# Conv of every second band's fourth channel block: diagonal half-channel weights in four array tiles instead of composite weights

## The chip, the cores and the metric

The kernel runs on one core of a Trainium2 chip. The time is device microseconds from launch to end; before the change the median of three runs is 3966.65 us (3966.45 to 3969.41). Engines: PE (matrix products, with PEld its weight loads), DVE (vector), ACT (activations and copies), POOL (GpSimd) and SP (DMA queue).

## The reference

One transformer-like layer on 16 images of 128 channels and 96 x 96 pixels, fp32: channel attention with a residual, then this feed-forward part with a residual.

```
xn2 = layernorm over channels of x
h1  = w_in (512 x 128) applied to each pixel of xn2
h2  = 3 x 3 depthwise conv of h1, 512 channels, zero padding
h3  = gelu(h2)
out = x + w_out (128 x 512) applied to each pixel of h3
```

## The kernel before

An image is cut into 8 bands of 12 rows (BR = 12), so there are 128 bands, numbered g. The 512 hidden channels are four blocks of 128 (n = 0 to 3). Channels lie on the 128 partitions, pixels along the free dimension. A normalised image lies in the ring `xn`, rows padded by one column.

A pair (g, n) is a job of `conv_job`, in the usual way: PE projects the rows into PSUM (`hidden`, L1162, mostly 4 rows or 384 columns at a time), ACT copies them into the padded buffer `h1s[n]` (`kept`, L1167), and the two rows that the next band needs are copied at the end (`halo`, L1158), so that they aren't projected twice. The nine taps are then shared out. ACT makes two to four products (L1178, tile `pr`); POOL adds one of them to the unscaled middle tap (`merge`, L1181) and issues DMAs that add another product to a product (L1203) and the rest to the result (L1206). DVE does the other taps as multiply-adds over 1152 pixels in the PSUM tile `acc` (L1194; L1190 the first and the last). ACT applies GELU (L1211) into `h3`.

For 45 of the 128 bands (`PE_BANDS`, `PE_LAST`) the fourth block (n = 3, `PE_CHUNK`) goes another way, `by_matmuls`: PE computes projection and conv at once from `xn`, with nine composite matrices `comp[:, t, :]` (w_in times the tap's weight, 128 x 128), for units of 4 rows: nine matmuls into one PSUM bank (L1274) and a small one of six rows that corrects the columns at the image's edge (L1280). ACT applies GELU from PSUM (L1292). These bands need no projection, copy or halo for n = 3.

`ffn_out` multiplies by w_out, four matmuls for 4 rows (L1315), and DVE adds them to x (L1322). Beside this run the norms and the attention of the next image: transposes (L868, L964), mixing (L818), Gram sums (L916), statistics on DVE (L876), scales on POOL (L881, L885, L909). All PE results but Gram and `acc` pass through four PSUM banks, `h_0` to `h_3`.

The order on each engine is fixed when the program is built. `Plan` gives each operation a place on a common axis of jobs (`at(kind, place)`, with offsets `AT`, and `SHIFTS` by stretch of 15 jobs) and costs in ns, and plays the work through; of the operations that are ready, each engine takes the one with the lowest place.

Of the kernel before, what the change touches and what calls it, by code (L numbers as in the profile page):

```python
# [21 lines left out]
PE_OF = 30
PE_LAST = (0, 1, 3, 4, 6)
# [28 lines left out]
    load_w=-385.3, weights=-616.15, zeros=-141.7, load_a=-42.4, forth_a=-588.2, stats_a=1671.35, variance_a=269.75,  # L52
    power_a=-755.3, pool_product=152.05, merge=-380.8, scaled_a=-1419.9, gram=1191.75, back_a=416.05,
    place_a=228.35, attention=-37, mix=1454.35, residual=-779.15, mixed=-33.8, add_x=-342.3, forth_b=1585.15,
    stats_b=614.45, variance_b=-1160.25, power_b=-1398.6, shift_b=20.9, scaled_b=-3615.05, back_b=417.3,
    place_b=-902.15, halo=4531.85, hidden=416.95, kept=-903.15, products=3487.6, add_last=-380.1, tap=10.85,
    add_first=-1420.85, gelu=4569.5, conv=1192.9, conv_gelu=10.15, out=421.1, add=612.75, store=75.2,
    mix_0=-440.15, residual_0=-785.8, mixed_0=-1036.75, add_x_0=-1518.55, gram_0=475.45, forth_a_0=-103.4,
    forth_b_0=-946.85, stats_a_0=-789.15, stats_b_0=-710.05, scaled_a_0=-915.5, copied_a=35.4, copied_b=-38.35,
    copied_a_0=-43.45, copied_b_0=1111, scaled_b_0=-128.2, back_a_0=485, back_b_0=-1340.55, place_a_0=-547.95,  # L60
    place_b_0=-708.95, shift_b_0=22.8, late=-293.55, load_a_0=-390.35, load_dw=-378, units=-654.05,
# [5 lines left out]
    0: dict(load_w=1.9, zeros=-8.4, load_a=-22.8, forth_a=-1.1, stats_a=-0.3, variance_a=-0.3, power_a=-8.1,
        merge=-300.7, gram=0.2, back_a=-0.2, place_a=-1660.1, attention=-276.4, mix=-21.7, residual=-23.2,
        mixed=530.5, forth_b=40.5, stats_b=-118.7, variance_b=14.1, power_b=605.1, back_b=0.1, place_b=1.6,
        halo=4.3, kept=986.6, products=-7.1, add_last=329.8, tap=-1.6, add_first=1.7, gelu=7.1, conv=-6,  # L70
        conv_gelu=0.4, out=0.2, add=-660.9, store=1.7, mix_0=-899, residual_0=-622, gram_0=0.9, forth_a_0=18.5,
        stats_a_0=-2.4, stats_b_0=19.6, scaled_a_0=-65.5, copied_a=-60.9, back_a_0=-6.5, back_b_0=0.2,
        place_a_0=399.7, place_b_0=1296.2, late=10.6, load_a_0=4.4, load_dw=229.6, units=8.6, variance_a_0=619.5,
        power_a_0=-469.8, variance_b_0=-341, power_b_0=-17.1),
    1: dict(load_a=-14.5, forth_a=0.1, stats_a=14.8, variance_a=1354, power_a=1176.9, merge=637, scaled_a=46.3,
        gram=-0.1, back_a=0.1, place_a=1.6, attention=-12.1, mix=-4.5, mixed=403.6, add_x=1946.3, forth_b=-6.6,
        stats_b=-1.9, variance_b=-52.3, power_b=5.8, back_b=170.3, place_b=-0.2, halo=-1066.6, hidden=-3.3,
        kept=923, products=1, add_last=-6.7, tap=0.7, add_first=1488, gelu=1.5, conv=0.7, conv_gelu=0.9, out=-0.4,
        add=2.8, copied_a=379.4),
    2: dict(forth_a=0.2, stats_a=-3.5, variance_a=-8.2, merge=0.8, scaled_a=-9.6, gram=3281.1, place_a=1229.9,  # L80
        mixed=38.9, forth_b=-125.8, stats_b=576.6, variance_b=-252.3, power_b=-0.5, back_b=-1367.9, place_b=-21.3,
        halo=-1033.7, kept=0.2, add_last=1838.5, add_first=19.2, gelu=-95.7, conv=-0.2, conv_gelu=0.1, add=-688.1,
        store=-2.9, copied_b=-10.5),
    3: dict(load_a=0.3, stats_a=-421.1, variance_a=1.7, power_a=1940.7, merge=360.1, scaled_a=19.9, gram=-3.7,
        back_a=-1.6, place_a=-1386.7, mix=-3.2, mixed=-1368.8, add_x=331.4, forth_b=9.5, stats_b=-631.1,
        power_b=84.1, place_b=-406.8, halo=-5.4, kept=976.7, products=0.3, add_last=0.8, tap=0.1, add_first=1358.3,
        gelu=2.1, conv=-2.9, conv_gelu=-0.3, add=-1929.6, store=-1489.9, copied_a=4.3),
    4: dict(load_a=-0.5, forth_a=0.4, stats_a=-0.7, power_a=24.6, merge=-2.2, scaled_a=1377.6, back_a=-152.2,
        place_a=-15.7, mixed=-9.8, add_x=2.6, forth_b=73.3, stats_b=12.2, variance_b=-15.1, power_b=-8.5,
        back_b=0.1, place_b=2076.2, halo=5, kept=185.5, products=-0.1, add_last=6.5, tap=0.5, add_first=-10.8,  # L90
        gelu=-13.4, conv=-3.1, conv_gelu=0.7, out=0.1, add=-664.4, store=1113.3, copied_a=-1138.6),
    5: dict(load_a=0.1, stats_a=-1.1, variance_a=-313.3, power_a=1.2, merge=-12.5, scaled_a=1035.8, gram=-3.2,
        back_a=-3.1, place_a=-265.5, attention=-0.6, mix=2.8, mixed=137.1, add_x=-6.9, forth_b=-29.6,
        stats_b=-638.6, variance_b=771.6, power_b=45, back_b=-404.6, place_b=146, halo=-0.5, kept=200.1,
        add_last=2.7, add_first=-1.7, gelu=-2, conv=0.4, conv_gelu=0.3, add=2.9, store=1134, copied_a=1.4,
        copied_b=18.3),
    6: dict(forth_a=-0.2, stats_a=15.7, variance_a=-46.9, power_a=976.2, scaled_a=-8.2, gram=2277.6, back_a=-2,
        place_a=-7.5, mix=0.1, mixed=-346.5, add_x=-1.2, forth_b=3.4, stats_b=0.2, variance_b=0.1, power_b=37.6,
        back_b=-0.5, place_b=1358.9, halo=49.9, kept=-465.7, products=-0.1, gelu=21, conv=-22.3, conv_gelu=0.1,
        add=-599.3, store=3342.4, copied_a=-381.6),  # L100
    7: dict(forth_a=0.2, stats_a=-1.6, variance_a=1309.9, power_a=2424.9, merge=0.2, scaled_a=4976.2, gram=-27.8,
        back_a=11.1, place_a=176.5, attention=-0.4, mix=0.7, mixed=-5.3, add_x=358.3, forth_b=7.9, stats_b=1.4,
        variance_b=-1.7, power_b=8.5, back_b=0.6, place_b=19.7, halo=1.9, kept=864.1, products=-1, add_last=342.7,
        tap=-0.6, add_first=15.3, gelu=5, conv=3346, conv_gelu=-0.5, store=1090.3, copied_a=-967.2,
        copied_b=1704.6),
    8: dict(load_a=-2.4, forth_a=1.3, stats_a=0.3, variance_a=-4.2, power_a=-4.3, merge=7.7, scaled_a=670.4,
        gram=2291.6, place_a=24.6, mix=-0.3, mixed=1600.2, add_x=-36.8, forth_b=57.3, stats_b=1042.9,
        variance_b=-17, power_b=-0.3, back_b=-0.2, place_b=2469.7, halo=-2888.4, kept=1099.2, add_last=-33.7,
        tap=0.8, gelu=-6.8, conv=-6.2, conv_gelu=0.9, out=0.1, add=-406.4, copied_a=2.7),
    9: dict(load_a=-1.9, stats_a=-0.2, variance_a=-0.1, power_a=23.8, merge=-25, scaled_a=11.3, gram=-7.9,  # L110
        back_a=-0.3, place_a=-511.8, attention=-1.8, mix=-2.4, mixed=-1119.9, add_x=320.8, forth_b=-16.7,
        stats_b=-566.6, variance_b=8.9, power_b=10.1, back_b=-0.2, place_b=-0.8, kept=-0.8, products=-0.3,
        add_last=-16.7, tap=0.3, add_first=6.8, gelu=19.2, conv=-5.3, conv_gelu=0.1, add=0.7, store=-980.3,
        copied_a=25.1),
    10: dict(forth_a=-0.1, stats_a=-18.6, variance_a=213.9, power_a=-1.6, merge=-0.3, scaled_a=1679, gram=3360.3,
        back_a=-0.8, place_a=-13.6, mix=-3.6, mixed=503.8, add_x=829.5, forth_b=1.4, stats_b=16.4,
        variance_b=1422.9, power_b=15, back_b=0.5, place_b=1532, halo=9, hidden=1.3, kept=1393.5, products=0.1,
        add_last=-363.1, add_first=-14.8, gelu=10.8, conv=0.2, out=67.7, store=-4.8, copied_a=-32.2,
        copied_b=-331.3),
    11: dict(forth_a=-0.7, stats_a=13.2, variance_a=367, power_a=5322.9, merge=-21.3, scaled_a=1837.4, gram=3416.9,  # L120
        back_a=-339.2, attention=-1, mix=-1.1, mixed=640.8, add_x=2.6, forth_b=4.6, stats_b=10.1, variance_b=-16.9,
        power_b=4.6, back_b=-0.2, place_b=565.6, halo=13.3, hidden=-0.7, kept=859.2, add_last=23.5, tap=0.7,
        add_first=-6.9, conv=1.5, conv_gelu=-0.2, add=1024.5, store=4493.9),
# [1276 lines left out]
```

## Time and profile before

| | us |
|---|---|
| median of three runs | 3966.65 |
| span of the profiled execution | 3974.3 |
| PE busy | 3892.4 |
| DVE busy | 3834.8 |
| ACT busy | 3558.1 |
| POOL busy | 3379.4 |

The profiled execution's own time is its span. PE's busy time counts matmuls whose ends are modelled and overlap, so that the pace of matmuls is read from their starts. Groups of the profile give an operation's line, output and inputs, shape, count, then busy time and mean ns of one, then the idle time before it and what ended it.

### The profile page before, as it was taken

The numbers are of one execution on the slowest core, as the hardware profiler recorded it, in microseconds if no ns is written. First come the engines' busy times: TensorE is split into PE (matmuls) and PEld (weight loads), VectorE is DVE, ScalarE is ACT, GpSimd is POOL, SyncE is SP. The second block draws the span as 40 slices with busy tenths as digits, with TensorE's granted clock in tenths as the row PEclk, the third lists the DMA queues.
The fourth block names the chain that finished last, engine by engine and source line by source line (L and its number), as shares of the span: only waits on it lengthen the run. The fifth ranks groups of instructions, "written<-read, shape, count | busy, mean of one in ns | idle before, by whom it ended". The sixth has DMA issues, their size and how long they took to land.

```text
span 3974.3 us, 50973 instructions
## 1 busy us (share of the span) xinstructions
PE 3892.4 (98%) x16760; PEld 2521.7 (63%) x16760; DVE 3834.8 (96%) x4390; ACT 3558.1 (90%) x5186; POOL 3379.4 (85%) x3107
## 2 busy tenths in 40 slices
PE   8999999999999999999999999999999999999999
PEld 7566666666666666666666666666666666665555
DVE  7999999999999999999999999999999999999998
ACT  3989989989999999999989989999899999998886
POOL 5998988898898988988888888888888888888674
PEclk9999999999999999999999999999999999999999
DMA  3999999999999999999999999999999999999996
GB/s 100 187 191 204 200 200 198 199 202 198 210 201 209 203 198 203 200 210 201 194 202 197 207 201 194 205 197 206 189 192 206 203 207 201 203 197 183 191 189 146
DMA packets 191691, 777.42 MB, mean 196 GB/s; under 512 B 22208, under 2 KB 23616, under 8 KB 191424
## 3 DMA queue, kind: packets, MB, share of 16 engines
q0 software_dynamic: 151920, 622.33, 82.6%
q1 hardware_dynamic: 38784, 151.75, 10.2%
q8 instruction: 132, 2.16, 0.2%
q14 instruction: 135, 1.11, 0.1%
q10 hardware_dynamic: 720, 0.07, 0.0%
HBM read 148.85 MB, written 75.50 MB: 56 GB/s over the span
## 4 chain that ended last, share of the span: by engine, by line
PE 58%; DVE 14%; ACT 10%; DMA 7%; POOL 6%; issue 5%; POOLq 0%; DVEq 0%; ACTq 0%
PE h L1315 15%; PE h L1162 14%; PE h L1274 13%; DVE acc L1194 6%; DMA h<-pr 5%; ACT pr L1178 5%; PE h L818 4%; PE h L964 4%; PE g L916 3%; PE h L868 3%; DVE acc L1190 3%; DVE h L1190 2%; ACT h L1167 2%; POOL merged L1181 2%; DMA pr<-pr 2%
## 5 line engine op out<-in xcount | busy, mean ns | idle before, releaser
L1178 ACT ACTIVATE pr<-h,ratio 128x1152 f32<-128x1152 f32 x1494 | 1837.2, 1271 | 37.6 <-DMA h<-pr 12.6
L1194 DVE SCALAR_TENSOR_TENSOR acc<-h,ratio,acc 128x1152 f32<-128x1152 f32 (+1 forms) x1308 | 1810.3, 1384 | 7.7
L1181 POOL TENSOR_TENSOR merged<-pr,h 128x1152 f32<-128x1152 f32 x466 | 1238.1, 2657 | 100.5 <-DVE acc L1190 54.7
L1162 PE MATMUL h<-xn,winT 128*128 128x384 f32 (+2 forms) x2802 | 1088.0, 496 | 16.0 <-ACT h L1167 9.2
L1315 PE MATMUL h<-h,woutT 128*128 128x384 f32 x3072 | 1086.2, 488 | 1.7 <-ACT h L1167 1.1
L1274 PE MATMUL h<-xn,comp 128*128 128x380 f32 (+2 forms) x2430 | 895.0, 482 | 2.2 <-ACT h L1167 1.5
L1167 ACT COPY h<-h 128x384 f32<-128x384 f32 (+2 forms) x1401 | 652.9, 493 | 192.4 <-PE h L1162 187.5
L1315 PEld LDWEIGHTS h<-h,woutT 128*128 128x128 f32 x3072 | 565.2, 190 | 359.3 <-ACT h L1167 7.8
L1162 PEld LDWEIGHTS h<-xn,winT 128*128 128x128 f32 x2802 | 500.0, 190 | 326.6 <-issue 34.2
L1190 DVE SCALAR_TENSOR_TENSOR acc<-h,ratio,merged 128x1152 f32<-128x1152 f32 x466 | 686.6, 1473 | 20.9 <-POOL merged L1184 10.1
L1206 POOL DMA_DIRECT2D h<-pr x466 | 463.3, 994 | 241.9 <-DVE h L1190 57.5
L1190 DVE SCALAR_TENSOR_TENSOR h<-h,ratio,acc 128x1152 f32<-128x1152 f32 x467 | 655.2, 1403 | 3.4
L1211 ACT ACTIVATE h<-h,ksum 128x1152 f32<-128x1152 f32 (+2 forms) x586 | 616.0, 1081 | 46.4 <-DMA h<-pr 45.6
L1274 PEld LDWEIGHTS h<-xn,comp 128*128 128x128 f32 x2430 | 430.6, 189 | 235.2 <-issue 17.1
L1203 POOL DMA_DIRECT2D pr<-pr x466 | 478.7, 1040 | 103.1 <-ACT pr L1178 73.4
L885 POOL TENSOR_TENSOR ve_b<-ve_b,mhalf 128x4 f32<-128x4 f32 x288 | 366.0, 1277 | 7.9
L909 POOL TENSOR_TENSOR zT<-zT,ve_a 128x512 f32<-128x512 f32 x270 | 331.3, 1232 | 8.6
L885 POOL TENSOR_TENSOR ve_a<-ve_a,mhalf 128x4 f32<-128x4 f32 x288 | 318.6, 1109 | 15.3
L868 PE MATMUL h<-ident,x 128*128 128x128 f32 x2244 | 317.0, 275 | 13.7 <-ACT xn L970 4.9
L868 PEld LDWEIGHTS h<-ident,x 128*128 128x128 f32 x2244 | 263.6, 142 | 96.4 <-issue 38.6
L818 PE MATMUL h<-xn,mwT 128*128 128x384 f32 x768 | 289.1, 490 | 7.7 <-ACT h L1167 3.2
L916 PEld LDWEIGHTS g<-zT 128*128 128x128 f32 x2160 | 269.9, 191 | 40.2 <-POOL zT L909 11.0
(190 smaller groups left out, 3967.0 us busy)
## 6 DMA issues: line engine op xcount, KB each, us to landing
pr<-pr POOLq DMA_DIRECT2D x466, 576.0 KB, 7.8
h<-pr POOLq DMA_DIRECT2D x466, 576.0 KB, 7.7
x<-in_x_dram SPq DMA_DIRECT2D x128, 576.0 KB, 7.5
out_dram<-x SPq DMA_DIRECT2D x127, 576.0 KB, 4.6
x<-in_x_dram POOLq DMA_DIRECT2D x123, 576.0 KB, 9.1
out_dram<-x SPq DMA_DIRECT2D x3, 192.0 KB, 1.9
h<-in_L_conv_w_in_dram SPq DMA_DIRECT2D x1, 256.0 KB, 3.4
h<-in_L_conv_w_out_dram SPq DMA_DIRECT2D x1, 256.0 KB, 3.6
```

Source lines behind the costliest of these rows:

```text
L868: nc.tensor.transpose(d["pT", q][:, k, :], xt[:, j * P : (j + 1) * P], ident)
L885: nc.gpsimd.tensor_tensor(rstd, rstd, mhalf, ALU.pow)
L1162: nc.tensor.matmul(rows(ph), lhsT=winT[:, n, :], rhs=window(xn, r0 + r, e - r, 1), start=True, stop=True)
L1167: nc.scalar.copy(window(h1_, r, e - r, 1), rows(d.pop(("ph", r))))
L1178: nc.scalar.activation(to, shifted(t), AF.Copy, scale=ratio[:, n, t : t + 1])
L1181: nc.gpsimd.tensor_tensor(merged, d["pr", dma_taps[0]], shifted(UNIT), ALU.add)
L1190: nc.vector.scalar_tensor_tensor(to, shifted(t), ratio[:, n, t : t + 1], also, ALU.mult, ALU.add)
L1194: nc.vector.scalar_tensor_tensor(to, shifted(t)[:, lo:hi, cut], ratio[:, n, t : t + 1], to, ALU.mult, ALU.add)
L1203: nc.gpsimd.dma_start(out=d["pr", dma_taps[1]], in_=d["pr", t], accum_op=ALU.add)
L1211: nc.scalar.activation(h3, h3, AF.Gelu, bias=ksum[:, z, n : n + 1])
L1274: nc.tensor.matmul(d["pc"][:, lo:hi, cut], lhsT=comp[:, t, :], rhs=window(xn, r0 + dy, UR, dx)[:, lo:hi, cut], start=(t == order[0]), stop ...
L1315: nc.tensor.matmul(rows(d["po"]), lhsT=woutT[:, n, :], rhs=h3s[g, n][:, s * UR : (s + 1) * UR, :], start=(k == 0), stop=(k == NCH - 1),)
```

## The change

`by_pe` now takes every second band (64 of 128: `PE_OF = 2`, the odd g). In those bands the fourth block is projected, copied and passed on by the halo copy like the others (kinds `hidden_p`, `kept_p`, `halo_p`); only the conv itself goes over PE. Its weights `diag` are diagonal, nine taps of 64 x 64 for each half of the channels. The array is used as four tiles of 64 rows and 64 columns: row half m is the half of the channels, column half q the half of the band's rows (q = 0 rows 0 to 5, q = 1 rows 6 to 11). In two steps (k) of 3 rows (288 columns) each tap takes four matmuls, (q, m) = (0, 0), (1, 1), (1, 0), (0, 1), into two PSUM banks, one for each m, so that a bank holds 64 channels of two row groups. GELU reads a bank (`ksum_pe` holds the bias in that layout), and `h3` of this block keeps the layout.

`ffn_out_pe` therefore starts a unit of 3 rows with matmuls on half the partitions (`wout_pe`, tiles of 64 x 128, one row half for each of two output banks) and then adds the other three blocks with full matmuls. The edge correction (L1280) and the composite matrices are gone. All offsets are new: `AT`, `TURN`, and `PHASES` by the band's place in the image, while `SHIFTS` is empty.

```diff
-PE_BANDS = (0, 3, 6, 9, 12, 15, 18, 21, 24, 27)
-PE_OF = 30
-PE_LAST = (0, 1, 3, 4, 6)
+PE_BANDS = (0,)
+PE_OF = 2
+HALF = 64
+PR = 3
...
-    comp = const.tile([P, 9, P], F32, name="comp")
+    diag = const.tile([P, 9, HALF], F32, name="diag")
...
+            pe(t_mm((e - r) * W), at("hidden" + pe_, jk), lambda r=r, e=e: hidden(r, e), [*zs, ("w", "in")], [ph, *to])
+            act(t_copy((e - r) * W), at("kept" + pe_, jk), lambda r=r, e=e: kept(r, e), [ph], to)
+        if pe_:
+            by_matmuls(j, g, h1)
+            if to_halo:
+                act(t_copy(2 * W), at("halo_p", j), halo, h1[3:], h1[:1])
+            return
...
+    def by_matmuls(p, g, h1):
+        order = (1, 0, 2)
+
+        def product(k, dy):
+            if dy == order[0]:
+                d["pc", k] = [rows(bank((g, "conv", k, m), PR * W)) for m in range(2)]
+            for dx in (1, 0, 2):
+                t = 3 * dy + dx
+                for q, m in ((0, 0), (1, 1), (1, 0), (0, 1)):
+                    r0 = 2 * PR * q + PR * k
+                    lo, hi, _ = inside(t, b * BR + r0, PR, True)
+                    of, to = slice(m * HALF, (m + 1) * HALF), slice(q * HALF, (q + 1) * HALF)
+                    nc.tensor.matmul(
+                        d["pc", k][m][to, lo:hi, :], lhsT=diag[of, t, :],
+                        rhs=window(h1s[PE_CHUNK], r0 + dy, PR, dx)[of, lo:hi, :],
+                        start=(t == UNIT), stop=(dy == order[-1] and dx == 2),
+                    )
...
+        def gelu(k, m):
+            for a, e, z in step_parts(k):
+                to = h3_of(g, PE_CHUNK)[:, 2 * PR * m + PR * k + a : 2 * PR * m + PR * k + e, :]
+                nc.scalar.activation(to, d["pc", k][m][:, a:e, :], AF.Gelu, bias=ksum_pe[:, z, m : m + 1])
...
+    def ffn_out_pe(p, g, k):
+        pos = [("h", ("out", g, q, k)) for q in range(2)]
+        r0s = [2 * PR * q + PR * k for q in range(2)]
...
+        def halves():
+            for m in range(2):
+                for q in range(2):
+                    of = slice(q * HALF, (q + 1) * HALF)
+                    r = 2 * PR * m + PR * k
+                    nc.tensor.matmul(
+                        rows(bank(pos[q][1], PR * W)), lhsT=wout_pe[of, m, :], rhs=h3s[g, PE_CHUNK][of, r : r + PR, :],
+                        start=(m == 0), stop=False,
+                    )
```

PE's order in the middle of the run, before: a unit of a band whose fourth block goes over PE. A row is line, operation, output and inputs (`x_...` and `ve_b...` belong to the norms, `mwT` to the mixing), shape and how many in a row.

```order
L1274 MATMUL h_3_76<-xn_128,comp_124 128x384
L1274 MATMUL h_3_76<-xn_128,comp_124 128x4x95
L818 MATMUL h_0_73<-xn_128,mwT_8_12948 128x384
L1274 MATMUL h_3_76<-xn_128,comp_124 128x4x95 x3
L818 MATMUL h_0_73<-xn_128,mwT_8_12948 128x384
L818 MATMUL h_2_75<-xn_128,mwT_8_12948 128x384
L1274 MATMUL h_3_76<-xn_128,comp_124 128x384
L1274 MATMUL h_3_76<-xn_128,comp_124 128x4x95
L1280 MATMUL h_3_76<-ident_78,edgeT_112 128x4x2
```

The composite matmuls of a unit, in one bank, are mixed with other work and close with the edge matmul. On PE after the change, at the second step of such a band's conv (L1094 is the projection, L1259 the full output products, L798 and L894 transposes, L846 the Gram sums):

```order
L1094 MATMUL h_0_73<-xn_127,winT_121 128x384
L1259 MATMUL h_2_75<-h3_6_159,woutT_122 128x384
L894 MATMUL h_3_76<-ident_78,ve_b7_8_14071 128x128 x3
L846 MATMUL g_8_13220<-zT_2_163 128x129 x4
L1094 MATMUL h_0_73<-xn_127,winT_121 128x384
L1094 MATMUL h_3_76<-xn_127,winT_121 128x384
L798 MATMUL h_1_74<-ident_78,x2_7_4_13962 128x128 x4
L1211 MATMUL h_2_75<-h1_3_143,diag_123 64x288
L1211 MATMUL h_0_73<-h1_3_143,diag_123 64x288
```

The two banks `h_2` and `h_0` then take 24 such matmuls without a break, one other operation, and the last 12; over the whole run there are 217 unbroken runs of 12, 24 or 36. On PE, at the output of that band (L1283 works on half the partitions):

```order
L748 MATMUL h_0_73<-xn_127,mwT_7_13212 128x384
L1283 MATMUL h_2_75<-h3_2_155,wout_pe_83 128x288
L1283 MATMUL h_1_74<-h3_2_155,wout_pe_83 128x288
L1283 MATMUL h_2_75<-h3_2_155,wout_pe_83 128x288
L1283 MATMUL h_1_74<-h3_2_155,wout_pe_83 128x288
L1259 MATMUL h_2_75<-h3_0_153,woutT_122 128x288
L1259 MATMUL h_2_75<-h3_7_160,woutT_122 128x288
L1259 MATMUL h_2_75<-h3_3_156,woutT_122 128x288
L1259 MATMUL h_1_74<-h3_0_153,woutT_122 128x288
```

Two output banks are now filled together, where `ffn_out` before filled one with four full matmuls. On ACT, after the change, around a band of the next image (L1110 products, L1227 the GELU of PE's blocks, L1143 that of the others, L1090 the halo copy; `h1_3` is the fourth block's buffer):

```order
L1110 ACTIVATE pr_1_146<-h1_1_141,ratio_106 128x1152
L1143 ACTIVATE h3_2_155<-h3_2_155,ksum_110 128x1152
L1090 COPY h1_2_142<-h1_2_142 128x2x96
L1227 ACTIVATE h3_0_153<-h_3_76,ksum_pe_111 128x288
L1055 COPY mwT_8_15033<-g_8_13220 128x128
L1056 COPY d_8_15035<-g_8_13220 128x1
L1227 ACTIVATE h3_0_153<-h_1_74,ksum_pe_111 128x288
L1090 COPY h1_3_143<-h1_3_143 128x2x96
L1110 ACTIVATE pr_4_149<-h1_1_141,ratio_106 128x1152
```

Each step's two banks are emptied by two GELUs, and the fourth block's halo copy, which before was left out beside a band that went over PE, now follows the first step. Over the run ACT's copies of projected rows go from 1401 to 1536, halo copies from 371 to 448, products from 1494 to 1437.

More of the change, by code (lines that the diff above doesn't have):

```diff
@@ L51 @@
 AT = dict(
[L52 to L61, printed above, removed]
@@ new lines @@
+    variance_b=2.39, power_b=2.49, shift_b=22.37, scaled_b=-3613.23, back_b=3.21, place_b=3.36, halo=6.59,
+    halo_p=8.94, hidden=3.5, hidden_p=5.31, kept_p=3.82, kept=1.97, products=10.49, add_last=6.26, tap=5.39,
+    add_first=6.31, gelu=7.45, conv=8.06, conv_gelu=8.64, out=6.8, add=7.23, store=5.08, mix_0=7.87,
+    residual_0=13.83, mixed_0=-1036.57, add_x_0=-1522.05, gram_0=11.4, forth_a_0=13.33, forth_b_0=4.32,
+    stats_a_0=15.56, stats_b_0=8, scaled_a_0=16.57, copied_a=-4.84, copied_b=3.43, copied_a_0=-42.25,
@@ new lines @@
+    copied_b_0=1111.46, scaled_b_0=-128.12, back_a_0=18.85, back_b_0=13.55, place_a_0=17.71, place_b_0=11.05,
+    shift_b_0=31.15, late=10.9, load_a_0=12.46, load_dw=15.58, units=9.96, variance_a_0=13.17, power_a_0=21.5,
+    variance_b_0=8.5, power_b_0=11.24,
+)
+TURN = dict(
+    load_w=-386.6, weights=-616.15, zeros=-121.87, load_a=-42.46, forth_a=-595.61, pool_product=152.05,
+    attention=-36.46, mix=1452.66, products=3498.48, tap=10.94, conv=13.45, conv_gelu=10.15, mix_0=-440.15,
+    forth_a_0=-103.4, load_a_0=-400.68,
+)
@@ L65 @@
 STRETCH = 15
 SHIFTS = {
[L67 to L123, printed above, removed]
-    12: dict(load_a=10.3, forth_a=5.5, stats_a=9.9, variance_a=-0.8, merge=-188.3, gram=0.1, place_a=-1371.9,
-        mix=-1.2, mixed=-1155.8, add_x=-847.4, forth_b=-21.3, stats_b=581.5, variance_b=21.3, power_b=-52.5,
-        place_b=1.1, halo=-3.3, kept=17.6, products=0.4, tap=1, add_first=9.7, gelu=14.3, conv=-0.1, out=-0.4,
-        add=959.9, store=-103.4, copied_a=-1417.6),
@@ L194 @@
-    29: dict(merge=964.3, mix=2.3, mixed=29.9, add_x=-554.8, forth_b=-404.1, stats_b=2866.7, variance_b=1165.5,
-        power_b=2005.5, back_b=-405.9, place_b=13.1, hidden=-0.1, kept=-2.5, products=-0.2, add_last=968.5,
-        gelu=-4545.7, conv=-5.1, conv_gelu=-1.8, out=170.1, add=-604.8, store=0.5, copied_b=3518.7),
-    30: dict(merge=0.3, mix=32.8, mixed=-2.3, add_x=956.2, forth_b=9.3, stats_b=-10.1, variance_b=787.8,
-        power_b=0.4, back_b=-0.3, place_b=-44.2, halo=-4106.2, kept=-4.5, products=-1.5, add_last=7.5,
-        add_first=-1.5, gelu=-14.8, conv=0.1, conv_gelu=-0.1, add=-2030, store=-448.6),
@@ L200 @@
-    31: dict(merge=4987, hidden=741.3, kept=1.8, products=1119.8, tap=1184.1, add_first=2628.9, gelu=-4553.7,
-        conv=9, conv_gelu=-2.6, out=4185.8, add=-1517.3, store=4532.1),
 }
-STEP = dict(scaled=0.3, hidden=0.1, products=0.5, tap=0.166, conv=1.6, conv_tap=0.03, out=0.8, out_part=0.05)
+STEP = dict(scaled=0.3, hidden=0.1, products=0.5, tap=0.166, conv=1.6, conv_tap=0.03, out=0.8, out_pe=1.2, out_part=0.05)
 SLACK = 150
@@ L477, in tile_restormer_block @@
     ksum = const.tile([P, 3, NCH], F32, name="ksum")
[L478 to L479 removed]
+    ksum_pe = const.tile([P, 3, 2], F32, name="ksum_pe")
     none = const.tile([P, 1], F32, name="none")
@@ L706, in keep_centred_in @@
                 nc.vector.tensor_mul(ksum[:, z, :], ksum[:, z, :], kn)
-                for side in range(2):
-                    to = edge[:, 2 * z + side : 2 * z + side + 1]
-                    nc.vector.tensor_reduce(to, ratio[:, PE_CHUNK, lo + 2 * side : hi : 3], AX.X, ALU.add)
-            nc.vector.tensor_scalar(edge, edge, kn[:, PE_CHUNK : PE_CHUNK + 1], -1.0, ALU.mult, ALU.mult)
-        def edges():
-            v["pe"] = bank(("weights", "edge"))[:6, :P]
-            nc.tensor.transpose(v["pe"], edge, ident)
-        def centred_conv(ts):
-            pc = v["pc4"] = bank(("weights", "centred conv", ts[0]))[:, : len(ts) * P]
-            nc.tensor.matmul(
-                pc, lhsT=centre, rhs=comp[:, ts[0] : ts[-1] + 1, :].rearrange("p t c -> p (t c)"), start=True, stop=True
-            )
+            for q in range(2):
+                for m in range(2):
+                    of, to = ksum[m * HALF : (m + 1) * HALF, :, PE_CHUNK], ksum_pe[q * HALF : (q + 1) * HALF, :, m]
+                    nc.vector.tensor_copy(to[:, :1], of[:, :1])
+                    nc.vector.tensor_copy(to[:, 1:2], of[:, 1:2] if not q else of[:, :1])
+                    nc.vector.tensor_copy(to[:, 2:], of[:, 2:] if q else of[:, :1])
         def unit_parts():
@@ L753, in weights @@
         dve(3300, at("late", p), keep_centred_in, pc + pk, [("w", "in")])
-        pk = [("h", ("weights", "edge"))]
-        pe(230, at("late", p), edges, [("w", "in")], pk)
-        dve(200, at("late", p), lambda: nc.vector.tensor_copy(edgeT, v["pe"]), pk, [("w", "conv")])
         transposed(
@@ L1148, in conv_job @@
         jn = (g, n)
-        from_halo = b > 0 and (n != PE_CHUNK or not by_pe(g - 1))
-        to_halo = b < NB - 1 and (n != PE_CHUNK or not by_pe(g + 1))
+        from_halo = b > 0
+        to_halo = b < NB - 1
+        pe_ = "_p" if j is None else ""
+        j = first[g] if pe_ else j
         h1_ = h1s[n]
@@ L1306, in ffn_out, with step_parts @@
-    def ffn_out(p, g, s):
+    def by_matmuls(p, g, h1):
         i, b = divmod(g, NB)
         d = {}
-        po = ("h", ("out", g, s))
-        order = sorted(range(NCH), key=lambda n: (n != PE_CHUNK, n))
-        def product(k, n):
-            if k == 0:
-                d["po"] = bank(("out", g, s), UT)
-            nc.tensor.matmul(
-                rows(d["po"]), lhsT=woutT[:, n, :], rhs=h3s[g, n][:, s * UR : (s + 1) * UR, :],
-                start=(k == 0), stop=(k == NCH - 1),
-            )
-        def add_here():
-            xt = x_unit(xbs, i, s + b * UPB)
-            nc.vector.tensor_add(xt, d["po"], xt)
-        def store(k, n):
-            at_ = slice(b * BR * W + k * UT, b * BR * W + (k + n) * UT)
-            nc.sync.dma_start(out=ov[i, :, at_], in_=xbs[i, b][:, k * UT : (k + n) * UT])
+        order = (1, 0, 2)
[12 more added lines that the diff above has]
+                        start=(t == UNIT), stop=(dy == order[-1] and dx == 2),
+                    )
+        def step_parts(k):
+            if b == 0 and k == 0:
+                return [(0, 1, 1), (1, PR, 0)]
+            if b == NB - 1 and k == 1:
+                return [(PR - 1, PR, 2), (0, PR - 1, 0)]
+            return [(0, PR, 0)]
+        def gelu(k, m):
+            for a, e, z in step_parts(k):
+                to = h3_of(g, PE_CHUNK)[:, 2 * PR * m + PR * k + a : 2 * PR * m + PR * k + e, :]
+                nc.scalar.activation(to, d["pc", k][m][:, a:e, :], AF.Gelu, bias=ksum_pe[:, z, m : m + 1])
+        for k in range(2):
+            pcs = [("h", (g, "conv", k, m)) for m in range(2)]
+            h3 = [("h3", (g, PE_CHUNK), k)]
+            for c, dy in enumerate(order):
+                pk = p + STEP["conv"] * k + STEP["conv_tap"] * c
+                pe(T_CONV, at("conv", pk), lambda k=k, dy=dy: product(k, dy), [*h1[k:], ("w", "conv")], [*pcs, *(h3 if not c else ())])
+            ns = sum(t_act((e - a) * W, 1) for a, e, _ in step_parts(k))
+            for m in range(2):
+                act(ns, at("conv_gelu", p + STEP["conv"] * k), lambda k=k, m=m: gelu(k, m), [pcs[m]], h3)
@@ new lines, in out_add, with add_here, store @@
+    def out_add(p, g, key, r0, n):
+        i, b = divmod(g, NB)
+        units = range(r0 // UR, (r0 + n - 1) // UR + 1)
+        xt = lambda: xbs[i, b][:, r0 * W : (r0 + n) * W]
+        def add_here():
+            nc.vector.tensor_add(xt(), banks[plan.slot[key]][:, : n * W], xt())
+        def store(r0, n):
+            at_ = slice((b * BR + r0) * W, (b * BR + r0 + n) * W)
+            nc.sync.dma_start(out=ov[i, :, at_], in_=xbs[i, b][:, r0 * W : (r0 + n) * W])
+        dve(t_dve(n * W), at("add", p), add_here, [key], [("xb", (i, b), s) for s in units])
+        if g == NG - 1:
+            move(at("store", p), lambda: store(r0, n), [("xb", (i, b), s) for s in units], [], T_MOVE * n / BR)
+        elif r0 + n == BR:
+            move(at("store", p), lambda: store(0, BR), [("xb", (i, b), k) for k in range(UPB)], [], T_MOVE)
@@ L1328, in ffn_out, with product_of, product @@
+    def product_of(po, g, n, r0, e0, start, stop):
+        nc.tensor.matmul(rows(po), lhsT=woutT[:, n, :], rhs=h3s[g, n][:, r0:e0, :], start=start, stop=stop)
+    def ffn_out(p, g, s):
+        po = ("h", ("out", g, s))
+        order = range(NCH)
+        def product(n):
+            product_of(bank(po[1], UT), g, n, s * UR, (s + 1) * UR, n == 0, n == NCH - 1)
         for k, n in enumerate(order):
             pk = p + STEP["out_part"] * k
-            pe(t_mm(UT), at("out", pk), lambda k=k, n=n: product(k, n), [*(("h3", (g, m), s) for m in (order if k == 0 else [n])), ("w", "out")], [po])
@@ L1331, in ffn_out @@
-        band_ = [("xb", (i, b), k) for k in range(UPB)]
-        dve(t_dve(UT), at("add", p), add_here, [po], [("xb", (i, b), s)])
-        if g == NG - 1:
-            move(at("store", p), lambda: store(s, 1), [("xb", (i, b), s)], [], T_MOVE / UPB)
-        elif s == UPB - 1:
-            move(at("store", p), lambda: store(0, UPB), band_, [], T_MOVE)
+            pe(t_mm(UT), at("out", pk), lambda n=n: product(n), [*(("h3", (g, m), s) for m in (order if k == 0 else [n])), ("w", "out")], [po])
@@ L1348, in tile_restormer_block @@
     band = len(jobs) / NG
+    own = {gn: j for j, gn in enumerate(jobs)}
     def job_of(g):
@@ L1362, in tile_restormer_block @@
         norm(i, True, lambda t: start2 + band * t / TPB)
-        for j, (g, n) in enumerate(jobs):
-            if g // NB == i:
-                conv_job(j, g, n)
         for g in range(NB * i, NB * (i + 1)):
+            for n in range(NCH):
+                conv_job(own.get((g, n)), g, n)
+            if by_pe(g):
+                for k in range(2):
+                    ffn_out_pe(first[g + 1] + STEP["out_pe"] * k, g, k)
+                continue
             for s in range(UPB):
-                if by_pe(g):
-                    by_matmuls(first[g] + STEP["conv"] * s, g, s)
                 ffn_out(first[g + 1] + STEP["out"] * s, g, s)
```

258 lines of the change are left out of this document (115 added, 143 removed).

## The prediction

> **What bounds the kernel now.** I read the page's totals first, then the windows, the waits and the groups by line.
>
> ```profile
> span 3974.3 us, 50973 instructions
> PE 3892.4 (98%) x16760; PEld 2521.7 (63%) x16760; DVE 3834.8 (96%) x4390; ACT 3558.1 (90%) x5186; POOL 3379.4 (85%) x3107
> ```
>
> Busy time per engine. The span leaves PE 82 us of idle time (3974 - 3892), DVE 139, ACT 416 and POOL 595. The profiled span is 8 us above the median of the runs (3966.65); I sum against the span and take 8 off at the end.
>
> ```profile
> 0.00:50.00 50.00, 42.13 (x311) 37.41 (x311) 35.87 (x112) 8.32 (x18) 23.41 (x72) 1.00 0.39 123
> 1500.00:2000.00 500.00, 494.77 (x2144) 322.78 (x2143) 492.62 (x552) 461.98 (x675) 439.21 (x399) 1.00 0.96 202
> 3900.00:3974.00 74.00, 70.77 (x229) 41.50 (x227) 58.80 (x51) 38.75 (x54) 25.33 (x18) 1.00 0.61 133
> ```
>
> Stretch, then busy time of PE, PEld, DVE, ACT, POOL, the granted clock and the DMA share. In the middle PE is busy 494.8 and DVE 492.6 of 500 us, at full clock: two engines are full at once, and only what relieves both shortens the run. Start and end are a small part.
>
> ```profile
> ACT h L1167 <- PE h L1162: 187.5, 242, 9.5
> PEld h L1280 <- issue: 71.7, 135, 0.5
> DVE x L1322 <- PE h L1315: 31.6, 37, 2.5
> ```
>
> Who waited for whom: total, times, longest. DVE's largest wait is for PE's output products, ACT's for PE's projection. So PE is the supplier, and time taken from DVE alone would turn into such waits.
>
> **The change, engine by engine.** Bands whose fourth block goes over PE rise from 45 to 64 (2430 instructions of L1274 are 1215 matmuls, 27 a band); DVE jobs fall from 467 to 448.
>
> ```profile
> L1194 DVE SCALAR_TENSOR_TENSOR acc<-h,ratio,acc 128x1152 f32<-128x1152 f32 (+1 forms) x1308 | 1810.3, 1384 | 7.7
> L1190 DVE SCALAR_TENSOR_TENSOR acc<-h,ratio,merged 128x1152 f32<-128x1152 f32 x466 | 686.6, 1473 | 20.9 <-POOL merged L1184 10.1
> L1190 DVE SCALAR_TENSOR_TENSOR h<-h,ratio,acc 128x1152 f32<-128x1152 f32 x467 | 655.2, 1403 | 3.4
> L1322 DVE TENSOR_TENSOR x<-h,x 128x384 f32<-128x384 f32 x384 | 211.6, 551 | 39.3 <-PE h L1315 31.6 <-ACT pr L1178 3.2 <-issue 1.7
> ```
>
> DVE: a fourth-block job has five taps, one of 1.473, three of 1.384, one of 1.403 us: 7.03, and 19 jobs give -133.5. The closing addition of 64 bands is cut into four of 288 columns instead of three of 384. The price of 288 lies between 0.413 (three quarters of 0.551) and 0.551; 0.45 keeps a fixed part, so 4 x 0.45 - 3 x 0.551 = +0.15 a band, +9 (0 to +35). Sum -124: DVE 3711.
>
> ```profile
> L1178 ACT ACTIVATE pr<-h,ratio 128x1152 f32<-128x1152 f32 x1494 | 1837.2, 1271 | 37.6 <-DMA h<-pr 12.6
> L1211 ACT ACTIVATE h<-h,ksum 128x1152 f32<-128x1152 f32 (+2 forms) x586 | 616.0, 1081 | 46.4 <-DMA h<-pr 45.6
> L1167 ACT COPY h<-h 128x384 f32<-128x384 f32 x1092 | 506.8, 488 | 144.8 <-PE h L1162 142.0
> L1158 ACT COPY h<-h 128x192 f32<-128x192 f32 x371 | 134.1, 378 | 0.1
> L1292 ACT ACTIVATE h<-h,ksum 128x384 f32<-128x384 f32 x124 | 72.8, 587 | 20.9 <-PE h L1280 20.3
> L1292 ACT ACTIVATE h<-h,ksum 128x288 f32<-128x288 f32 x11 | 5.8, 528 | 0.0
> ```
>
> ACT, by busy time over count: 57 products fewer at 1.23, -70; 19 GELUs at 616.0/467 = 1.32 a job, -25; 135 more copies of projected rows at 0.464, +63; 77 more halo copies at 0.361, +28; the GELU of PE's blocks goes from some 83 us (146 calls) to 64 x 4 x 0.53 plus split edge rows, about 145, +62. Sum +58: ACT 3616. It lies in the 416 us that ACT has free; what becomes later is PE's next tap group where a copy is late.
>
> ```profile
> L1181 POOL TENSOR_TENSOR merged<-pr,h 128x1152 f32<-128x1152 f32 x466 | 1238.1, 2657 | 100.5 <-DVE acc L1190 54.7
> L1203 POOL DMA_DIRECT2D pr<-pr x466 | 478.7, 1040 | 103.1 <-ACT pr L1178 73.4
> L1206 POOL DMA_DIRECT2D h<-pr x466 | 463.3, 994 | 241.9 <-DVE h L1190 57.5
> ```
>
> POOL: 19 merges and 38 accumulating DMAs fewer, 19 x 4.69 = -89, and its DMA queue carries 38 fewer transfers. Worth nothing by itself, since neither is full.
>
> PE needs the real pace of a matmul, start to start, since its busy times overlap:
>
> ```profile
> 2007.60 1.46 PE L818 MATMUL h<-xn,mwT 128*128 128x384 f32 x4
> 2008.89 1.13 PE L1274 MATMUL h<-xn,comp 128*128 128x288 f32 x4
> 2009.89 0.91 PE L818 MATMUL h<-xn,mwT 128*128 128x384 f32 x2
> ...
> 2016.72 0.97 PE L1162 MATMUL h<-xn,winT 128*128 128x480 f32 x2
> 2017.53 0.80 PE L1274 MATMUL h<-xn,comp 128*128 128x380 f32 x2
> 2018.26 0.60 PE L1280 MATMUL h<-ident,edgeT 6*128 6x2 f32 x4
> 2018.79 0.91 PE L1315 MATMUL h<-h,woutT 128*128 128x384 f32 x2
> 2019.54 0.65 PE L1162 MATMUL h<-xn,winT 128*128 128x288 f32 x2
> 2020.03 3.39 PE L1315 MATMUL h<-h,woutT 128*128 128x384 f32 x10
> ```
>
> Start, length, group. A matmul is two instructions. Four instructions of 384 columns last 1.29 us (2007.60 to 2008.89), so 0.645 a matmul; one of 288 lasts 0.49 (2019.54 to 2020.03), one of 480 0.81. The edge matmul uses six rows of the array, and around it the pace breaks: 2017.53 + 0.64 is 2018.17, but it starts at 2018.26, and the pair after it takes 0.75 instead of 0.645. A change of array shape costs 0.09 + 0.10 = 0.19 us there and back. The edge instructions themselves come 0.133 apart (0.53/4).
>
> ```profile
> L1274 PE MATMUL h<-xn,comp 128*128 128x380 f32 (+2 forms) x2430 | 895.0, 482 | 2.2 <-ACT h L1167 1.5
> L1280 PEld LDWEIGHTS h<-ident,edgeT 6*128 6x128 f32 x292 | 41.9, 183 | 71.7 <-issue 71.7
> L1162 PE MATMUL h<-xn,winT 128*128 128x384 f32 x2184 | 845.1, 492 | 12.7 <-ACT h L1167 6.5 <-DVE xn L968 1.6 <-DVE st_b L876 1.3
> L1162 PE MATMUL h<-xn,winT 128*128 128x480 f32 x384 | 181.0, 568 | 2.1 <-ACT h L1167 1.6 <-ACT x L827 0.5
> L1162 PE MATMUL h<-xn,winT 128*128 128x288 f32 x234 | 76.6, 411 | 1.2 <-ACT h L1167 1.1
> L1315 PEld LDWEIGHTS h<-h,woutT 128*128 128x128 f32 x3072 | 565.2, 190 | 359.3 <-ACT h L1167 7.8 <-issue 7.5 <-DVE xn L968 1.6
> L1044 PEld LDWEIGHTS g<-wqkT,gs 128*1 128x1 f32 x30 | 2.5, 83 | 0.8
> ```
>
> - Composite conv goes: 1215 x 0.64 = -778. Edges go: 292 x 0.133 + 135 x 0.19 = -64.
> - Projection: counts of 384/480/288 columns go from 1092/192/117 to 1280/128/128: +121 - 52 + 5 = +75.
> - Output: 768 matmuls of 384 columns become 768 of 288 (full) and 512 of 288 on half the rows: -768 x 0.645 + 768 x 0.49 + 512 x 0.245 = +6 if two halves run side by side, +131 if not.
> - New conv: 64 bands x 2 steps x 9 taps = 1152 taps, each four matmuls of 288 columns, one per quarter of the array. No row of before has two matmuls at once, so the price of a tap has two ends: 0.49 if the four stream side by side, 4 x 0.49 = 1.96 if one after the other. I take 0.55. The four use different rows or columns, and their outputs different banks or partitions. The loads decide next: a load of 128 columns takes 190 ns and one of 1 column 83, so a column costs 0.84 ns and 64 columns 54 ns; eight loads a tap are 0.43 us, under 0.49. With the 24 ns by which an edge instruction exceeds its own load (133 - 109) they are 0.62 if none hides behind a stream. 0.55 is the middle of 0.49 and 0.62. 1152 x 0.55 = +634.
> - Array shape: 217 unbroken runs of the quarter form and 128 of the half form, 345 x 0.19 = +66 (0 to +66, since a run of quarters needs no second drain where a half form follows).
>
> PE's sum: -778 - 64 + 75 + 6 + 634 + 66 = -61, so 3831. The preparation of weights loses three rounds at the start and gains one; I cost that at nothing (0 to -5), since the first 100 us wait on loads and statistics as well.
>
> **The sum.** If PE keeps its 82 us of idle time: 3831 + 82 = 3913. If DVE keeps its 139: 3711 + 139 = 3850. Both are ends of the same answer: DVE's waits for L1315 shrink when PE is ahead, PE's waits grow as both get scarce. The middle is 3881; less 8, 3873 us, 2.4% faster. Its own range is 3800 (0.49 a tap, DVE's idle time down to 100) to 3930.
>
> **Rivals.**
> - *Loads not hidden.* A tap takes 0.60 to 0.65: +58 to +115 on PE. With all 82 us idle that is 3963 to 4020 after the 8 are off; with 50 idle, 3931 to 3988. For it speaks the edge row, whose loads stood idle before (71.7 us in 135 waits); against it that PEld is busy 63% beside a PE of 98%. The sum crosses no change at 0.60 to 0.62. By the Trainium skill ("TensorE: Matmul & The Clock Gate", Part 3), four row tiles gained 3.07 times; by it a tap would be 1.96/3.07 = 0.64 and the sum 4009. No run here shows that.
> - *Passes in program order (slower).* Each matmul is two instructions on the same quarter. If a matmul may not start before the one ahead has started, the second pass waits for the first, and the next quarter waits behind it: 0.245 a matmul, 0.98 a tap, +495 on PE, 3831 + 495 + 82 - 8 = 4400. For it: in the timeline PE's groups never overtake, and the two passes are neighbours. Against: nothing shows that a pass for another quarter must queue behind. The same page of the Trainium skill states it as strict order of start and end; no row of before has two tiles to test it on.
> - *One after the other.* 1.96 a tap, +1624 and +125 for the halves: 5654. The change would not do what it says. It would take a path that all quarters share, and no row speaks for one.
> - *Banks.* A conv step holds two of the four PSUM banks for 9 x 0.55 = 5 us, 128 times, where a composite unit held one. ACT already waits 242 times for the projection, 0.77 us each. One such wait of PE in each step adds 99: 4004. Some of it gives 3930 to 4010.
>
> **Chances.** The forecast's case 0.66; loads 0.10; banks 0.09; program order 0.10; one after the other 0.03; something else 0.02. I call 0.2% (8 us, 3959 to 3975) what a measurement can tell from no change. Faster: the first case, half the banks and a little of the loads, 0.72; same 0.05; slower 0.23. The range 3800 to 4030 holds the first three cases and leaves out program order and worse.
>
> **What would show it.** Quarter matmuls: taps 0.5 to 0.6 us apart confirm the main step, 1.0 the program order. DVE's busy time should be near 3711, ACT's 3616, POOL's 3290, whatever the time. If PE's busy share falls below 95% with DVE waiting on the output products, it is the banks or the order. If PE is full and the time is above 3966, the tap's price was wrong.

## The result

The changed kernel takes 4077.6 us (4074.2 to 4079.1) against 3967.8 beside it: 1.0274 times as long, interval 1.0259 to 1.0288. I had forecast 3873 and a range of 3800 to 4030. It is slower, and outside the range.

The page of the changed kernel, span and busy time per engine:

```profile
span 4072.5 us, 66398 instructions
PE 3881.2 (95%) x24534; PEld 2513.4 (62%) x24534; DVE 3776.6 (93%) x4355; ACT 3579.4 (88%) x5459; POOL 3340.5 (82%) x3050
```

PE, DVE and POOL are busy less than before, ACT 21 us more, and yet the span is 98 us longer: PE's idle time went from 82 to 191 us, DVE's from 139 to 296. In the middle of the run (stretch, busy PE, PEld, DVE, ACT, POOL, clock, DMA share) no engine is as full as before:

```profile
1500.00:2000.00 500.00, 482.40 (x3070) 312.52 (x3071) 468.10 (x538) 452.06 (x693) 426.07 (x382) 1.00 0.91 190
```

Before, these were 494.8 for PE, 492.6 for DVE, and 0.96 for the DMA share. The new conv itself is fast. PE's timeline (start, length, group):

```profile
2033.10 4.60 PE L1211 MATMUL h<-h,diag 64*64 64x288 f32 x72
2037.63 1.56 PE L748 MATMUL h<-xn,mwT 128*128 128x384 f32 x4
...
2041.06 1.24 PE L1283 MATMUL h<-h,wout_pe 64*128 64x288 f32 x8
2042.23 2.21 PE L1259 MATMUL h<-h,woutT 128*128 128x288 f32 x8
```

72 instructions, nine taps of four matmuls, take 4.53 us with the change of shape: 0.503 a tap, where one full-array matmul of 288 columns took 0.49 before. So the four stream side by side. This is the longest kind of run; over the whole trace, 50 runs have nine taps (median 0.503 a tap), 67 have six (0.512) and 100 have three (0.539). That is 0.485 a tap and 0.16 us a run for the change of shape. Four half matmuls of the output take 1.17 us, 0.29 each with the change of shape.

These waits grew (total, times, longest; the first two lines are from before the change):

```profile
ACT h L1211 <- DMA h<-pr: 45.6, 37, 4.9
POOL merged L1181 <- ACT pr L1178: 28.6, 20, 3.5
...
ACT h L1143 <- DMA h<-pr: 142.9, 123, 5.8
POOL merged L1113 <- ACT pr L1110: 140.1, 97, 4.9
POOL ve_a L811 <- DVE st_a L806: 84.3, 46, 7.4
DVE x L1246 <- PE h L1259: 70.3, 83, 4.2
```

ACT's GELU waited 45.6 us for the accumulating DMA before, 142.9 now; POOL's merge waited 28.6 us for ACT's product, 140.1 now; DVE's closing addition 31.6 for PE, 70.3 now. Not all waits grew: ACT's largest, for PE's projection, fell from 187.5 to 147.9 us, and the merges wait 23.3 us for DVE instead of 54.7, so that all idle time before them went from 100.5 to 174.4:

```profile
L1113 POOL TENSOR_TENSOR merged<-pr,h 128x1152 f32<-128x1152 f32 x447 | 1169.6, 2616 | 174.4 <-ACT pr L1110 140.1
```

The accumulating DMAs themselves did not get slower. From issue to landing (last number, median us) they took, before and after:

```profile
h<-pr POOLq DMA_DIRECT2D x466, 576.0 KB, 7.7
...
h<-pr POOLq DMA_DIRECT2D x447, 576.0 KB, 7.6
```

One wait of the GELU on ACT's timeline:

```profile
2040.43 0.37 ACT L1090 COPY h<-h 128x192 f32<-128x192 f32 x1
2042.55 1.26 ACT L1143 ACTIVATE h<-h,ksum 128x1152 f32<-128x1152 f32 x1 [1.74 <-DMA h<-pr]
2043.71 0.84 ACT L1099 COPY h<-h 128x384 f32<-128x384 f32 x2
2044.58 3.55 ACT L1110 ACTIVATE pr<-h,ratio 128x1152 f32<-128x1152 f32 x3
```

For 1.74 us ACT stands at a GELU whose DMA has not landed. Behind it in the fixed order stand two copies that empty PSUM banks and three products for POOL. My reading is that no engine is short of time, that each meets its next instruction too early, and that the waits go round; a single wait like this one does not show it.

### The profile page after: what moved, and what is told of

It reads as the page before. It is cut to its first block, busy times and chain, and to the rows that moved or that the text cites. A ratio compares the mean times of both kernels' runs of the same rounds, so it can differ in the third digit from the quotient of the medians.

```text
span 4072.5 us, 66398 instructions
## 1 busy us (share of the span) xinstructions
PE 3881.2 (95%) x24534; PEld 2513.4 (62%) x24534; DVE 3776.6 (93%) x4355; ACT 3579.4 (88%) x5459; POOL 3340.5 (82%) x3050
## 4 chain that ended last, share of the span: by engine, by line
PE 26%; DMA 14%; POOL 12%; DVE 11%; ACT 11%; issue 6%; POOLq 0%; DVEq 0%; ACTq 0%
PE h L1259 8%; DMA h<-pr 7%; PE h L1094 7%; DVE acc L1126 5%; ACT pr L1110 4%; DMA pr<-pr 4%; POOL merged L1113 3%; PE h L1211 3%; DMA x<-in_x_dram 3%; ACT h L1099 2%; DVE acc L1122 2%; PE h L1283 2%; PE h L748 2%; DVE h L1122 2%; ACT h L1143 2%
## 5 line engine op out<-in xcount | busy, mean ns | idle before, releaser
L1110 ACT ACTIVATE pr<-h,ratio 128x1152 f32<-128x1152 f32 x1437 | 1791.0, 1286 | 10.5 <-POOL merged L1116 1.9
L1126 DVE SCALAR_TENSOR_TENSOR acc<-h,ratio,acc 128x1152 f32<-128x1152 f32 (+1 forms) x1251 | 1737.4, 1389 | 19.3
L1113 POOL TENSOR_TENSOR merged<-pr,h 128x1152 f32<-128x1152 f32 x447 | 1169.6, 2616 | 174.4 <-ACT pr L1110 140.1
L1094 PE MATMUL h<-xn,winT 128*128 128x384 f32 (+2 forms) x3072 | 1184.8, 500 | 51.2 <-ACT h L1099 17.5
L1259 PE MATMUL h<-h,woutT 128*128 128x384 f32 (+1 forms) x3072 | 988.4, 456 | 14.0 <-ACT h L1143 6.8
L1099 ACT COPY h<-h 128x384 f32<-128x384 f32 (+2 forms) x1536 | 717.6, 502 | 155.4 <-PE h L1094 147.9
L1094 PEld LDWEIGHTS h<-xn,winT 128*128 128x128 f32 x3072 | 539.5, 192 | 392.4 <-issue 58.3
L1259 PEld LDWEIGHTS h<-h,woutT 128*128 128x128 f32 x3072 | 557.3, 192 | 303.3 <-issue 79.6
L1143 ACT ACTIVATE h<-h,ksum 128x1152 f32<-128x1152 f32 (+3 forms) x562 | 591.4, 1078 | 149.1 <-DMA h<-pr 142.9
L1211 PE MATMUL h<-h,diag 64*64 64x288 f32 x9216 | 614.9, 406 | 0.9 <-DVE st_b L806 0.4
L1211 PEld LDWEIGHTS h<-h,diag 64*64 64x64 f32 x9216 | 340.9, 132 | 233.9 <-issue 44.5
L798 PE MATMUL h<-ident,x 128*128 128x128 f32 x2244 | 337.6, 277 | 40.7 <-DMA x<-in_x_dram 22.5
L798 PEld LDWEIGHTS h<-ident,x 128*128 128x128 f32 x2244 | 264.4, 141 | 163.2 <-issue 50.2
L1246 DVE TENSOR_TENSOR x<-h,x 128x288 f32<-128x288 f32 (+1 forms) x448 | 220.5, 494 | 85.4 <-PE h L1259 70.3
```

The costliest lines, as they stand in the source:

```text
L798: nc.tensor.transpose(d["pT", q][:, k, :], xt[:, j * P : (j + 1) * P], ident)
L1094: nc.tensor.matmul(rows(ph), lhsT=winT[:, n, :], rhs=window(xn, r0 + r, e - r, 1), start=True, stop=True)
L1099: nc.scalar.copy(window(h1_, r, e - r, 1), rows(d.pop(("ph", r))))
L1110: nc.scalar.activation(to, shifted(t), AF.Copy, scale=ratio[:, n, t : t + 1])
L1113: nc.gpsimd.tensor_tensor(merged, d["pr", dma_taps[0]], shifted(UNIT), ALU.add)
L1126: nc.vector.scalar_tensor_tensor(to, shifted(t)[:, lo:hi, cut], ratio[:, n, t : t + 1], to, ALU.mult, ALU.add)
```

## The experiments

The theories: O, the loss is the new order, not the new conv; B, the conv's pairs of banks and lumps of PE work make the waits in any order; and the forecast's own, that PE's work binds. D says that no order fitted to the planner's costs helps. L and P are finer versions of O (one cost of the planner is wrong), and N says that it is chance which order comes out.

**e1: the old kernel without its fitted offsets.** Only the order differs from before.

```diff
-SHIFTS = {0: dict(load_w=1.9, ...), ...}
+SHIFTS = {}
```

> The kernel before with its table SHIFTS emptied: the same work, only the order on the engines differs (offsets AT and RANK stay, the fitted offsets by stretch of 15 jobs are gone). Theory O (the loss of the change is its order): the fitted offsets are worth about as much as the change lost beside its lower load, so this kernel takes 4020 to 4070 us, with PE and DVE both idle longer (DVE busy near 94%). Theory B (the new conv's double banks and lumps of PE work make the waits, whatever the order): the old form loses little without its fit, 3965 to 4000 us.

4031.7 us, 1.0158 (1.0140 to 1.0176): 63 us for the order alone, with the same instructions. Its page:

```profile
span 4030.7 us, 50889 instructions
PE 3916.2 (97%) x16760; PEld 2525.3 (63%) x16760; DVE 3838.9 (95%) x4390; ACT 3563.7 (88%) x5186; POOL 3374.5 (84%) x3107
```

As O expected, but for DVE's 95% where I had 94%. PE's busy time rose by 24 us with the same work: busy time depends on the order too.

**e2: the changed kernel with offsets fitted to the planner's schedule.** `AT`, `TURN`, `PHASES` and a filled `SHIFTS`, chosen by trial so that the planned end comes earlier.

> The changed kernel, the same instructions, with other offsets (AT, TURN, PHASES and a SHIFTS table by stretch), found by trial so that the planner's own schedule ends 51 us earlier. Theory O: about that much comes back, 4010 to 4040 us, and the idle time of PE and DVE falls by some 50 us each. Theory B: banks and lumps stay, 4060 to 4085 us. Theory D (durations on the chip differ from the planner's costs, so that no order fitted to the planner helps): 4070 or more.

4056.2 us, 1.0221 (1.0205 to 1.0237). 21 us came back, where the plan had promised 51. The time lies just below B's range and misses O's; PE's idle time stayed (190 us), DVE's fell by 27. ACT's wait for the DMA stayed:

```profile
ACT h L1086 <- DMA h<-pr: 145.8, 113, 5.8
```

Of what an order gains on the planner's durations, well under half came back on the chip here.

**e3: the changed kernel with a third of the taps.**

```diff
-            for dx in (1, 0, 2):
+            for dx in (1,):
...
-                        start=(t == UNIT), stop=(dy == order[-1] and dx == 2),
+                        start=(t == UNIT), stop=(dy == order[-1]),
```

> The changed kernel with the middle column of taps only in the conv over PE (three of nine taps are multiplied, six left out); the order is the same. It takes 768 x 0.50 = 384 us of work off PE. If the kernel were bound by PE's work (forecast), it would fall by most of that until DVE binds, to 3870 to 3920 us. Theory O: PE waits for others in a fixed order as they wait for it; half or less comes back, 3930 to 4020 us.

4091.0 us, 1.0306 (1.0288 to 1.0325): with 6 of 9 taps gone it is 13 us slower, not faster. Both ranges are missed: I had expected O to give some of it back.

```profile
PE 3621.4 (89%) x18390; PEld 2303.6 (56%) x18390; DVE 3775.2 (92%) x4355; ACT 3573.2 (87%) x5459; POOL 3341.0 (82%) x3050
```

PE is idle for 469 us, and nothing is gained by it. So PE's work does not bind the changed kernel, and the forecast's view of it is refuted. The mean granted clock of the core fell from 0.990 to 0.971 as PE stood more, which may account for some of the 13 us:

```profile
core 0: 4090.0 us, clock 0.971
```

**e4, e5, e6: the planner's costs.** The offsets are those of the changed kernel. Work and tables stay; the order that the plan makes of them changes. `T_LAND` is changed in e4 and e6, the other two in e5 and e6.

```diff
-T_LAND = 1000
+T_LAND = 1800
-T_CONV = 1800
+T_CONV = 1560
...
-        pe(2 * t_mm(PR * W), at("out", p), halves, reads, pos)
+        pe(2 * t_mm(PR * W) + 190, at("out", p), halves, reads, pos)
```

> The changed kernel with one number of its planner changed: a DMA's landing is planned 0.8 us later (T_LAND 1000 to 1800). Work and offsets are the same; only the fixed order of the engines comes out differently. Theory L (the order of the changed kernel places the consumers of the accumulating DMAs at the planned landing; on the chip they land later, ACT and then everyone stands): ACT's wait of 143 us for h<-pr falls by half or more and the time by some 40 us, to 4020 to 4050 us. Theory N (any order that is not fitted loses about the same, and this one is as unfitted as the other): 4065 to 4090.

4064.2 us, 1.0240 (1.0225 to 1.0255): 13 us less instead of 40, which misses L's range and lies just below N's. ACT's wait for the DMA fell by a third, 49 us, of which the time shows a quarter:

```profile
ACT h L1143 <- DMA h<-pr: 93.5, 72, 6.3
```

> The changed kernel, planned with what the trace shows for its new PE work: three taps 1560 instead of 1800 ns, the four half matmuls of an output 1170 instead of 980 ns. Theory P (the plan holds PE's new groups for longer than they take, so that the order is laid out for a PE that is fuller than it is): some 40 us fall off, 4020 to 4050. Theory L alone: the late DMAs stay as they are, 4060 to 4085.

4050.3 us, 1.0202 (1.0186 to 1.0217): 27 us less instead of 40, just past the end of P's range.

> Both edits of the planner's costs together, the same offsets. L and P together: about 80 us, 3985 to 4015 us. If it is chance which order comes out (theory N): anywhere from 4020 to 4090, not ordered by the edits.

4035.7 us, 1.0169 (1.0152 to 1.0186): 42 us less than the changed kernel, 13 + 27 and 2 more. The parts add up, which speaks for L and P. But the time misses their range (3985 to 4015) and lies in that of chance (4020 to 4090), one order was made by each edit, and e2's offsets brought 21 us with no change of cost. So chance is not excluded. Of ACT's wait a third is left, while POOL's wait for products did not move:

```profile
POOL merged L1113 <- ACT pr L1110: 145.3, 97, 5.4
...
ACT h L1143 <- DMA h<-pr: 45.3, 41, 5.1
```

**e7: an order with slack.** The costs of e6 but for `T_CONV`, 1600 instead of 1560 (other DMAs 0.8 us later as well), and offsets fitted anew. A trial order was rated by a replay: each engine keeps its sequence, while DMAs land late by a random amount and POOL's work is slower.

> The changed kernel with other offsets and the planner's costs of e6 (other DMAs 0.8 us later too). The offsets were fitted anew by replaying each planned order, kept fixed, with DMAs that land late by a random amount and slower POOL work, so that an order counts only if it bears delays. Theory O+L (all of the loss is the order, and what an order needs is slack before the consumers of DMAs and products): 3930 to 3965 us, so faster than before the change, and DVE and PE busy above 96% of the span. Theory B (the new conv's double banks and lumps cost time in any order): not under 4000 us.

3962.2 us against 3970.6, 0.9978 (0.9969 to 0.9987): the same instructions as the changed kernel, 115 us less, and as fast as the kernel before or 0.2% faster. Theory B as stated is refuted: it asked for 4000 or more. A smaller cost of the banks is not excluded, since 3962 is still 89 us above the forecast of 3873.

```profile
span 3956.6 us, 66403 instructions
PE 3845.5 (97%) x24534; PEld 2501.0 (63%) x24534; DVE 3754.9 (95%) x4355; ACT 3575.7 (90%) x5459; POOL 3338.8 (84%) x3050
```

The same two waits (total, times, longest):

```profile
POOL merged L1056 <- ACT pr L1053: 96.2, 67, 3.9
...
ACT h L1086 <- DMA h<-pr: 42.8, 41, 4.3
```

Both waits of the result are lower, and the engines' idle time fell by 80 (PE) and 94 us (DVE). DVE is at 95%, not the 96 that I had expected. New offsets, costs and the rating by delays came together, so that the run does not show which of them did it.

**e8: e7 with a third of the taps**, the edit of e3.

> e7's order with three of nine taps in PE's conv (six left out), 384 us of PE work less, as in e3 against the changed kernel. If e7 is bound by a fixed order that holds all engines at once: within 15 us of e7. If PE's work binds once the order has slack: 30 us or more below e7.

3964.2 us, 0.9982 (0.9972 to 0.9991), 2 us from e7, with a granted clock of 0.978 for 0.995. PE's work is no bound in the good order either:

```profile
PE 3592.2 (91%) x18390; PEld 2286.1 (58%) x18390; DVE 3751.0 (95%) x4355; ACT 3571.8 (90%) x5459; POOL 3340.0 (84%) x3050
```

## Why the prediction was wrong

*The price of a tap* was right, on the low side: 0.50 measured, 0.55 taken, 0.49 the lower end. Even with the changes of shape, the new conv took 594 us where the sum had 634 and 41. The loads are hidden, so the rival "loads not hidden" is out. So is "program order", which asked for 0.98, and with it, for these tiles, the strict order of starts that I cited from the Trainium skill ("TensorE: Matmul & The Clock Gate", Part 3): two passes of one matmul do not hold up another tile. In the trace, in the run shown above, the first passes of the four start at 2033.100, .107, .113 and .120 us and the second passes from 2033.393 on, though the program has the two passes of a matmul next to each other. The factor of 3.07 in the same part of the Trainium skill, given for four tiles of 32 rows and 512 columns, is too low for these; 4 x 0.49 / 0.503 is 3.9.

*The counts* were right: bands, jobs, copies, DMAs. *Busy times* were off in one direction for PE, DVE and POOL: 3881 measured for 3831, 3777 for 3711, 3341 for 3290. The sums were made of durations by counts, but the busy time of an engine is a union in which the tail of one instruction lies under the next, and it grows when instructions stand apart. e1 against before (PE +24 with the same work) shows it for PE. So do four groups of PE that the change leaves alone (transposes and mixing, the same counts): they were busy for 963 us before and for 1014 after. For DVE the durations of all instructions add up to 4152 us before and 4040 after, -112 for the forecast -124, but their overlap fell from 318 to 264; for POOL to 3952 and 3858, -94 for -89, with the overlap down from 573 to 518. ACT came out at 3579 for 3616 by luck: its durations rose by 95, not 58, and its overlap by 74.

*The step that failed is the sum.* I let each engine keep its idle time of before, 82 us for PE and 139 for DVE, and took the middle. That idle time was the product of an order fitted to the old work, not a property of the kernel. The change replaced the whole order, which the front of the text said and the sum did not price. e1 gives the size that such a thing can have: 63 us in the old kernel, from a table of offsets. The changed order lost 115 us against e7's. With the idle times of the changed kernel put in place of the old ones, 3831 + 191 and 3711 + 296 give 4022 and 4007. What is missing to 4072 is the 50 and 66 us by which the busy times were too low.

*The first reading* was wrong in the same way. A PE at 98% and a DVE at 96% I took for two bounds of which the scarcer decides. e3 and e8 leave out two thirds of the taps, PE's busy time falls by 260 and 253 us, and nothing is gained. For the kernel before, no run took work from PE, so that its bound stays open. I take what binds the changed kernel to be a ring of fixed sequences: ACT's products, POOL's merges and DMA issues, the landing, ACT's GELU, PE's output, DVE's addition. That is argued, not shown: no run took work from DVE or the DMA engines. The forecast also called POOL's DMA queue not full, while the DMA share in its own row was 0.96. In e7 (stretch, busy PE, PEld, DVE, ACT, POOL, clock, DMA share) DVE and the DMA engines remain as rivals for the bound:

```profile
1500.00:2000.00 500.00, 490.43 (x3194) 321.89 (x3193) 478.98 (x548) 461.18 (x705) 436.46 (x392) 1.00 0.93 197
```

*The rival "banks"* had nearly the right symptom (PE at 95.3%, just not below the 95% that it names, DVE waiting on the output products) and a price of up to 4010. It is not the cause of the 115 us: e7 has the same two banks per step and 215 unbroken runs of matmuls for 217. It may hold part of the 89 us that e7 lies above the forecast. My test for the symptom named "the banks or the order", and only the banks had been a rival with a chance.

What is shown: order alone makes 63 us in the old kernel and 115 in the new, and two thirds of PE's taps none. The two corrected costs of the planner came with 13 and 27 us less; that they are the cause is not shown. What is open: the 73 us between e6 and e7, and the 89 us from e7 to the forecast. It is not shown either that the new conv is worth more than the composite one, since the old kernel's order could be fitted for slack too, which was not tried on the chip.

## What to carry to other kernels

Where all engines run fixed sequences near 95%, the order is a term of the sum like any other. When a change replaces it, price the idle time anew (here 60 to 115 us, 1.6 to 2.9%) instead of carrying it over, and give "slower by the order" its own chance. A schedule that is tight on assumed durations can lose on the chip where the assumption is early. What e4 to e7 suggest, without separating it, is to leave room in front of each consumer of a DMA, and to check the planner's costs of a new operation against its first trace before fitting offsets to them. To learn whether an engine binds, take some of its work away and keep the order: a nearly full engine is not yet a bound.
